# A two-level Strassen MLP: VectorE leaves its results in a free block, GpSimd adds them afterwards, and the weights' second sums are spread over the first group

## The chip, the cores and the metric

The kernel runs on one NeuronCore of a Trainium2 chip. The core has a matrix engine (TensorE, PE in the profile; PEld is its weight load), a vector engine (VectorE, DVE), a scalar engine (ScalarE, ACT), a general engine (GpSimd, POOL) and a queue that issues transfers (SyncE, SP). Each engine takes its instructions in the order in which the program has them, and they meet through semaphores. The metric is device time in microseconds (us); lower is better.

## The reference

A transformer block with cross attention, all in float32: 8 batches of 256 tokens, width 512, 16 heads, an MLP of 2048. Cut to what matters here:

```python
hidden = attention(layer_norm(x), ctx) @ cproj_w + cproj_b + x     # not touched by the change
y = layer_norm(hidden, ln2_w, ln2_b)
y = gelu(y @ fc_w + fc_b, approximate=True)    # fc_w: 512 x 2048
y = y @ proj_w + proj_b                        # proj_w: 2048 x 512
return hidden + y
```

## The kernel before, in words

**Tiling.** The 2048 tokens are four groups (`g` = 0 to 3) of 512. The attention of all groups comes first and leaves the hidden states in `hid_dram`; behind it the MLP runs group by group: for each, the fully connected layer with its GELU (tiles `pf`, results in `h`), then the projection (tiles `py`). Both parts are written out by hand: `manual_schedule` keeps every engine's instructions in the order of the source, so a line's place is its place in the queue of its engine.

**Strassen's form (with Winograd's sums).** A product of two 2 x 2 block matrices is done with seven block products in place of eight. A's sums are s1 (it is stored in the place of "21"), s2, s3, s4; B's are t1, t2, t4 and one in the place of "12". With P(a, b) for a block product: u1 = P(11,11); quarter 11 = u1 + P(12,21); u2 = u1 + P(s2,t2); u3 = u2 + P(s3,12); quarter 22 = u3 + P(21,t1); quarters 12 and 21 are u2 or u3 plus the products P(22,t4) and P(s4,22). `A_SUMS` and `B_SUMS` (summed up by L171) make the sums; `QI` gives the place of each of the seven operands in a tile.

**Group 0** uses one level. Its weights lie in four tiles `fcw[0]` to `fcw[3]`, one for each quarter `q` of the MLP's columns. For each `q`, seven `fc` products on TensorE go into PSUM banks 1, 6, 7, 5; VectorE adds make u2, u3 and the blocks of `h`, ScalarE the GELUs, and GpSimd the first two sums of `h` (`sum_h`, "s3" and "s2"). `sum_up(GP, fcw[q + 1], ...)` makes the next quarter's weight sums, `some_pw` takes steps of the generator `sum_pw`, which makes the projection weights' sums on VectorE (16 adds, 128x512 each).

**Groups 1 to 3** use two levels: each of the seven outer products is itself done with seven `sub` products of four matmuls, 128 tokens wide. An outer product `k` needs the weight operand `FC_ORDER[k][0]` as seven inner operands: these lie in `w2_dram` and are loaded to one of four tiles `w` by `load_w2`, four outer products ahead (the first four of group 1 during `py` of group 0). What has to be made for `w2_dram`, from the tiles `fcw` of group 0: the four raw inner quarters of each operand, which `keep_quarters` stores (from all seven operands at once, one transfer for each q and c, L982), and the four inner sums, which `split_sums` makes: four adds of 128x256 on VectorE or GpSimd into one of three slots of the tile `w_stage`, then two stores (L973, L974). A slot is taken again when its stores have landed. There are 14 such calls: seven operands, r = 0 (from `fcw[0]` and `fcw[2]`) and r = 1 (from `fcw[1]` and `fcw[3]`). The tile of the tokens' inner sums (`split_y`) has the same place as `w_stage`.

**The outer sums of groups 1 to 3.** `product(k, base, to)` makes four blocks, "11", "12", "21", "22", and puts them into `h[to]`, adding the blocks of `h[base]` if there is a base. For the three blocks that also get an inner u2 or u3, GpSimd first adds base and u into `h[to]` (`prepare`), and VectorE then adds the bank to that (`made`). Bank 5 is used twice in a product: `made("22")` reads it, and then `sub(5, "s4", "22", False, True)` adds to it; so TensorE can't start the latter before `made("22")` is done. After product 4, `both_to` adds whole parts of `h` to one another, half on GpSimd, half on VectorE. `h` has a fifth part, "s3": it holds the sums h11 - h21 from `sum_h("s3")` on, and in the fully connected layer of groups 1 to 3 nothing is in it.

**GELUs of groups 1 to 3.** `gelu` puts eight ScalarE instructions of a quarter into a list, and `some_gelus` issues two of them after each `sub`; ScalarE also copies u1 out of bank 1 (L1188).

**Projection, and the next group.** In `py` seven `proj` products of 32 matmuls use bank 1, 7, 1, 6, 1, 5, 7. Between them stand the next group's layer norm (`seen`, `roots`, `normalise`; L194 to L203), its transposes (`turn_next`, tile `pyt`), its sums and `split_y`; in group 0 also the second half of `split_sums` and the first `load_w2`. All adds by the helper `add` have line L927, all its matmuls L924: they are told apart by their tiles.

Of the kernel before, what the change touches and what calls it, by code (L numbers as in the profile page):

```python
# [16 lines left out]
P = 128  # L17
# [5 lines left out]
def tile_xattn_block(  # L23
# [45 lines left out]
    nc = tc.nc  # L69
# [16 lines left out]
    HI, HC, HF, HD2 = INNER // 2, NC // 2, NF // 2, D // 2  # L86
# [30 lines left out]
    at, col_of = 0, []  # L117
# [131 lines left out]
    with ExitStack() as att:  # L249
# [513 lines left out]
        g = 1  # L763
# [142 lines left out]
    with ExitStack() as mlp:  # L906
# [19 lines left out]
        def add(eng, to, a, b, op=ALU.add):  # L926
            eng.tensor_tensor(to, a, b, op)  # L927
# [9 lines left out]
        def sum_pw():  # L937
# [18 lines left out]
        w2_dram = tc.dram_tile([7, P, 7, HI // 2], F32, name="w2_dram")  # L956
        stage = wpool.tile([P, 3, 4, S], F32, tag="y2", bufs=1, name="w2_stage")
        FC_ORDER = (
            ("11", "11"), ("12", "21"), ("21", "t1"), ("s2", "t2"), ("s3", "12"), ("s4", "22"), ("22", "t4")
        )  # L960
        stages = [0]

# [11 lines left out]
            nc.sync.dma_start(to[:, 4:7, :], st[:, 1:, :])  # L974

        def keep_quarters(q):
            r = q % (NQF // 2)
            for c in range(HC):
                if q < NQF // 2 or c:
                    i = c if q < NQF // 2 else 3  # L980
                    to = w2_dram.rearrange("n p i s -> p n i s")[:, :, i, r * S : (r + 1) * S]
                    nc.sync.dma_start(to, fcw[q].t[:, :, c, :])  # L982

        w2 = {}

        def load_w2(g, k):
            t = wts.tile([P, 7, HC, S], F32, tag="w", bufs=4, name=f"w2_{g}_{k}")
            t = t.rearrange("p i h s -> p i (h s)")
            nc.sync.dma_start(t, w2_dram[QI[FC_ORDER[k][0]]])
            w2[g, k] = t  # L990

        y2s = {}
# [15 lines left out]
        for g in range(NG):  # L1008
# [39 lines left out]
            if g == 0:  # L1048
                y = ys[g]

                def fc(bank, w, b, q, first, last):
                    for i in range(2):
                        for c in range(HC):
# [5 lines left out]
                                last and c == HC - 1,  # L1059
                            )  # L1060

                for q in range(NQF):
# [16 lines left out]

                    def some_pw(n):  # L1080
                        if q:
                            for _ in range(n):
                                next(pw_sums)

                    ahead = q + 1 < NQF
                    fc(bank[1], "11", "11", q, True, False)
                    nc.scalar.copy(u1, bank[1])
                    fc(bank[6], "s2", "t2", q, True, True)
                    add(V, u2, bank[6], u1)
                    fc(bank[7], "s3", "12", q, True, False)  # L1090
                    add(V, u3, bank[7], u2)
                    fc(bank[5], "21", "t1", q, True, False)
                    add(V, x["22"], by_h(bank[5]), by_h(u3))
                    if ahead:
                        sum_up(GP, fcw[q + 1], A_SUMS, 0, 1)
                    some_pw(1)
                    fc(bank[1], "12", "21", q, False, True)

                    gelu("11", 0, by_h(bank[1]))
                    gelu("22", 1, x["22"])  # L1100
                    fc(bank[7], "22", "t4", q, False, True)
                    add(V, x["12"], by_h(bank[7]), by_h(u2))
                    if ahead:
                        sum_up(GP, fcw[q + 1], A_SUMS, 2, 3)
# [4 lines left out]
                    some_pw(1)  # L1109
# [6 lines left out]
                    if q == 2:  # L1116
                        split_sums(V, "11", 0)
                        split_sums(V, "12", 0)
                        for k in range(3):
                            keep_quarters(k)  # L1120
                    if q == 3:
                        split_sums(V, "21", 0)
                        split_sums(GP, "s2", 0)
                        split_sums(V, "s3", 0)
                        split_sums(GP, "s4", 0)
                        split_sums(V, "22", 0)
                        keep_quarters(3)
                        bias_ht()
            else:
                gelus = []  # L1130

                def some_gelus(n=2):
                    for f in gelus[:n]:
                        f()
                    del gelus[:n]
# [17 lines left out]
                def product(k, base, to):  # L1153

                    wt, yn = w2[g, k], QI[FC_ORDER[k][1]]
                    bank = {}
# [6 lines left out]
                    def sub(n, w, b, first, last):  # L1163
                        if first:
                            bank[n] = bank_of(n, f"pf{n}_{k}").rearrange("p i (j s) -> p (i j) s", j=2)
                        for m in range(HF // 2):
                            mm(
                                bank[n][:, m, :],
                                wt[:, QI[w], ts(m, P)],
                                y_of(b),  # L1170
                                first and m == 0,
                                last,
                            )
                        some_gelus()

                    def u(n):
                        return us(n, f"u{n}_{k}").rearrange("p i (j s) -> p (i j) s", j=2)

                    def prepare(cd, x):
                        if base:  # L1180
                            add(GP, block(to, cd), block(base, cd), x)

                    def made(cd, n, x):
                        add(V, block(to, cd), bank[n], block(to, cd) if base else x)

                    sub(1, "11", "11", True, False)
                    u1 = u(1)
# [4 lines left out]
                    prepare("21", u2)  # L1192
                    prepare("12", u2)
# [3 lines left out]
                    prepare("22", u3)  # L1197
# [3 lines left out]
                    if base:  # L1201
                        add(V, block(to, "11"), bank[1], block(base, "11"))
                    else:
                        nc.scalar.copy(block(to, "11"), bank[1])
                    sub(7, "22", "t4", False, True)
                    made("21", 7, u2)
                    sub(5, "s4", "22", False, True)
# [3 lines left out]
                    elif g + 1 < NG:  # L1211
                        load_w2(g + 1, k - 3)

                def both_to(to, x):

                    for eng, cd in ((GP, "21"), (V, "22"), (GP, "12"), (V, "11")):
                        add(eng, block(to, cd), block(to, cd), block(x, cd))


                product(0, None, "21")  # L1220
                product(1, "21", "11")
                gelu("11", 0)
                ht = residual(work, hid_dram[g], "resm", f"resm_{g}")
                load_next()
                product(2, None, "22")
                product(3, "21", "21")
                product(4, "21", "12")
                both_to("21", "22")
                both_to("22", "12")
                product(5, "21", "21")  # L1230
                gelu("21", 0)
                gelu("22", 1)
                product(6, "12", "12")
                some_gelus(len(gelus))
                gelu("12", 1)
                for which in ("s3", "s2"):
# [31 lines left out]
            u1, u2, u3 = (us(n, f"v{n}") for n in (1, 2, 3))  # L1268
            proj(bank[1], "11", "11", True, False)
            add(V, u1, bank[1], by_tiles(projb[:, HD2:]))  # L1270
            if g:
                some_gelus(HF)
            if g + 1 < NG:
                seen, roots, normalise = layer_norm(hids[g + 1], f"m{g + 1}")
# [6 lines left out]
                for f in normalise:  # L1281
                    f()
            if g == 0:
                split_sums(V, "11", 1)
                split_sums(GP, "12", 1)
                load_w2(1, 0)
                load_w2(1, 1)
            proj(bank[1], "12", "21", False, True)
            o_add(V, 0, 0, bank[1])
            for q in range(NQF):  # L1290
# [1 line left out]
            turn_next(0)  # L1292
            turn_next(1)
            if g == 0:
                split_sums(V, "21", 1)
                split_sums(GP, "s2", 1)
# [5 lines left out]
            turn_next(2)  # L1302
            turn_next(3)
            if g == 0:
                for n in ("s3", "s4", "22"):
                    split_sums(GP, n, 1)
                load_w2(1, 2)
                load_w2(1, 3)
# [57 lines left out]
```

## Time and profile before

| What | us |
|---|---|
| median of 3 runs (809.61 to 810.27) | 810.21 |
| the profiled execution | 808.85 |
| its span, from first to last instruction | 807.0 |
| TensorE busy (share of the span) | 755.3 (94%) |
| GpSimd busy | 473.0 (59%) |
| VectorE busy | 443.7 (55%) |
| ScalarE busy | 299.3 (37%) |
| attention, first `pf` matmul of group 0 at | 355.3 |
| `pf` of group 0, `py` of group 0 | 355.3 to 403.4, to 461.6 |
| `pf` of group 1, `py` of group 1 | 461.8 to 526.6, to 576.7 |
| `pf` of group 2, `py` of group 2 | 576.7 to 640.0, to 690.9 |
| `pf` of group 3, `py` of group 3 | 690.9 to 752.3, to 807.0 |

In a group of the profile, the name before `<-` is the tile written, those after it are read; then come the shape, the count, the busy time and the mean duration in ns, and behind the last bar the time the engine stood idle just before these instructions and what ended it. The page counts a float32 matmul as two records. The granted clock is a share of TensorE's full clock. A line of the time-ordered view has the start, the duration of the merged piece, engine and line, and in brackets the idle time before it with its releaser.

### The profile page before, as it was taken

Reading aid. Unit: us, or ns where it says so; the run is one execution under the profiler, and the core shown is the slowest. Engines: PE = TensorE matmul, PEld = TensorE weight load, DVE = VectorE, ACT = ScalarE, POOL = GpSimd, SP = SyncE. Lnnn points to the kernel's source line nnn. Section 1 sums busy time; section 2 is a strip of 40 time slices with the busy share of each in tenths; the row PEclk is TensorE's granted clock in tenths of the full one; section 3 lists DMA queues with packets and bytes.
Section 4 is the critical chain, followed back from the end, with each engine's and each line's share of the span. In section 5 each row is a group of like instructions: output and inputs, shape, how many; then the busy total and the mean of one; then the engine's idle time right before and its main releaser. Section 6 shows DMA issues by size and latency. Waiting matters only on the chain.

```text
span 807.0 us, 13477 instructions
## 1 busy us (share of the span) xinstructions
PE 755.3 (94%) x4941; PEld 648.0 (80%) x4941; DVE 443.7 (55%) x1085; ACT 299.3 (37%) x867; POOL 473.0 (59%) x431
## 2 busy tenths in 40 slices
PE   9999999999999999999979978799987899997997
PEld 8887777878888777788868877788987788886886
DVE  4667656755565668553779654553546353545111
ACT  3186777657767777504300012320020500021300
POOL 3866879486544789965468714594035671125940
PEclk9999999999999999999999999899998799998999
DMA  9525223713242584259395789520276400360001
GB/s 299 201 93 171 95 92 105 238 58 102 92 162 84 178 266 140 79 153 317 100 311 170 269 307 368 183 92 1 64 294 255 169 15 3 141 235 1 1 1 52
DMA packets 76449, 120.17 MB, mean 149 GB/s; under 512 B 5940, under 2 KB 59488, under 8 KB 73568
## 3 DMA queue, kind: packets, MB, share of 16 engines
q1 hardware_dynamic: 76128, 119.29, 43.4%
q8 instruction: 39, 0.64, 0.3%
q14 instruction: 26, 0.21, 0.1%
q0 software_dynamic: 256, 0.02, 0.0%
HBM read 85.48 MB, written 33.82 MB: 148 GB/s over the span
## 4 chain that ended last, share of the span: by engine, by line
PE 76%; POOL 10%; DVE 8%; DMA 2%; ACT 2%; issue 2%; SPq 0%; DVEq 0%; POOLq 0%
PE pf L924 18%; PE py L924 18%; POOL h L927 7%; PE ppt L625 6%; PE pqT L367 6%; PE pv L367 5%; PE po L367 5%; PE s L572 5%; PE pkT L367 4%; PE av L641 4%; POOL w_stage L927 2%; PE pkT L464 2%; DVE h L927 2%; DVE w_stage L927 1%; ACT pr L600 1%
## 5 line engine op out<-in xcount | busy, mean ns | idle before, releaser
L924 PE MATMUL pf<-y,w 128*128 128x128 f32 x1176 | 151.8, 294 | 38.2 <-DVE h L927 27.7
L924 PEld LDWEIGHTS pf<-y,w 128*128 128x128 f32 x1176 | 147.5, 208 | 42.4 <-DVE h L927 30.8
L614 POOL TENSOR_TENSOR pr<-pr,rsum 128x512 f32<-128x512 f32 x128 | 130.2, 1048 | 75.8 <-DVE rsum L612 44.5
L600 ACT ACTIVATE pr<-pr,nmax 128x256 f32<-128x256 f32 x256 | 128.1, 503 | 61.4 <-DVE nmax L590 61.2
L927 POOL TENSOR_TENSOR h<-h,u 128x512 f32<-128x512 f32 x45 | 55.7, 1267 | 146.3 <-DVE u L927 146.3
L590 DVE CUSTOM_DVE_ANT_0 pr<-s,mb 128x256 f32<-128x256 f32 x256 | 94.1, 413 | 42.0 <-PE s L572 35.0
L924 PE MATMUL py<-pw,h 128*128 128x256 f32 x384 | 89.0, 392 | 4.6 <-DVE v L927 4.6
L1188 ACT COPY u<-pf 128x512 f32<-128x512 f32 x21 | 12.2, 582 | 214.5 <-PE pf L924 214.5
L924 PEld LDWEIGHTS py<-pw,h 128*128 128x128 f32 x384 | 75.5, 198 | 15.7 <-DVE v L927 5.0
L924 PE MATMUL py<-pw_t,h 128*128 128x256 f32 x384 | 84.3, 379 | 0.0
L924 PEld LDWEIGHTS py<-pw_t,h 128*128 128x128 f32 x384 | 72.6, 190 | 10.0 <-DVE pw_t L927 0.3
L625 PEld LDWEIGHTS ppt<-ident,pr 128*128 128x128 f32 x512 | 57.3, 141 | 14.8 <-issue 9.5
L625 PE MATMUL ppt<-ident,pr 128*128 128x128 f32 x512 | 68.7, 276 | 0.2
L927 DVE TENSOR_TENSOR h<-pf,h 128x512 f32<-128x512 f32 x60 | 38.7, 686 | 52.0 <-POOL h L927 45.6
L1139 ACT ACTIVATE h<-h,cols 128x256 f32<-128x256 f32 x96 | 39.9, 497 | 66.5 <-DVE h L927 66.5
L927 POOL TENSOR_TENSOR h<-h,h 128x512 f32<-128x512 f32 x44 | 58.0, 1349 | 5.8 <-issue 4.7
L927 DVE TENSOR_TENSOR u<-pf,u 128x512 f32<-128x512 f32 x50 | 34.5, 690 | 40.8 <-PE pf L924 34.4
L630 ACT COPY pt<-ppt 128x512 f32<-128x512 f32 x96 | 51.6, 570 | 4.9 <-PE ppt L625 4.9
L367 PE MATMUL pv<-vw,ctxT 128*128 128x256 f32 x224 | 52.4, 380 | 0.0
L367 PE MATMUL pqT<-xnT,qw 128*128 128x256 f32 x224 | 51.0, 379 | 0.0
L924 PE MATMUL pf<-y,fcw 128*128 128x256 f32 x224 | 48.5, 379 | 0.0
L600 ACT ACTIVATION_READ_ACCUMULATOR pr<-pr,nmax 128x1 f32 x256 | 48.5, 189 | 0.0
(140 smaller groups left out, 1163.9 us busy)
## 6 DMA issues: line engine op xcount, KB each, us to landing
w<-w_dram SPq DMA_DIRECT2D x21, 1792.0 KB, 7.7
w_dram<-w_stage SPq DMA_DIRECT2D x14, 384.0 KB, 2.7
w_dram<-fcw SPq DMA_DIRECT2D x6, 896.0 KB, 9.1
ctx<-in_ctx_dram SPq DMA_DIRECT2D x16, 256.0 KB, 4.9
x<-in_x_dram SPq DMA_DIRECT2D x16, 256.0 KB, 4.5
v_dram<-st_v SPq DMA_DIRECT2D x16, 256.0 KB, 2.2
v<-v_dram SPq DMA_DIRECT2D x16, 256.0 KB, 3.5
resx<-in_x_dram SPq DMA_DIRECT2D x16, 256.0 KB, 5.1
```

Of the source, the lines that this page charges most:

```text
L367: nc.tensor.matmul(bank[n][:, i, :], l[:, c, ts(i, P)], r[:, c, :], start=first and i == 0 and c == 0, stop=last and c == HC - 1, skip_gro ...
L464: nc.tensor.matmul(bank[:, i, :], w[f"{n[0]}{j + 1}"][:, c, ts(i, P)], x()[f"{j + 1}{n[1]}"][:, c, :], start=at == 0, stop=j == 1 and c == ...
L572: nc.tensor.matmul(banks[j][:, i, :], qT[j * HD : (j + 1) * HD, b * S + i * P : b * S + (i + 1) * P], kT[j * HD : (j + 1) * HD, b * SK : ( ...
L590: nc.vector.tensor_tensor_reduce(pr[:, j, i, :], banks[j][:, i, :], mbias[g][1][:, b, :], scale=-SCALE, scalar=FLT_MAX, op0=ALU.add, op1=A ...
L600: nc.scalar.activation(pr[:, j, i, :], pr[:, j, i, :], AF.Exp, bias=nmax[:, j, i : i + 1], scale=-1.0, accum_out=sums[:, j, i : i + 1],)
L614: nc.gpsimd.tensor_tensor(pr[:, j], pr[:, j], rsum[:, j, :, None].to_broadcast([P, NQ, SK]), ALU.mult,)
L625: nc.tensor.transpose(ps[:, kc, ts(i, P)], probs[n][:, j, i, ts(kc, P)], ident)
L630: nc.scalar.copy(pt, ps)
L641: nc.tensor.matmul(av[j * HD : (j + 1) * HD, :], vs[g, hg][:, b * NK + kc, ts(j, HD)], pts[n, j][:, kc, :], start=(kc == 0), stop=(kc == N ...
L924: nc.tensor.matmul(ps, lhsT, rhs, start=first, stop=last, skip_group_check=True)
L927: eng.tensor_tensor(to, a, b, op)
L1139: nc.scalar.activation(h[n][:, :, p, :], h[n][:, :, p, :], AF.Gelu_apprx_tanh, bias=col(c_fcb, half * HF + p), scale=1.0,)
```

## The change

- `product` no longer adds base and u ahead. For the blocks "12", "21", "22" VectorE adds the bank and u into `r`, one of four slots of `h["s3"]`, and GpSimd afterwards adds `r` and the base to the target, for each of a list of (target, base) pairs. So u2 and u3 are read by VectorE alone. Block "11" is still added by VectorE, from the bank, once for each pair. Where a product has no base (product 0), the blocks go to the target as before.
- The order of the outer products is another, such that each result is the one before plus one product: 21 = P0; 11 = 21 + P1; 21 += P2; 12 = 21 + P3; 22 = 12 + P4 and 21 += P4; 21 += P5; 12 += P6. `both_to` falls away. Product 2, which had no base, now has one.
- `some_gelus` issues three at a time, and stands behind u2, behind u3, ahead of each `made` and ahead of block "11"; it no longer stands between the first `sub` and the copy of u1.
- The 14 `split_sums` are placed anew: ten in quarters 2 and 3 of group 0, after u2, u3 and the third block of a quarter (table `SPLITS`; six of the ten on GpSimd, four on VectorE), four in `py` of group 0. Before, seven were at the ends of quarters 2 and 3 and seven in `py`.
- The weight sums `A_SUMS` of `fcw[1]` and `fcw[2]` are made in quarter 0, those of `fcw[3]` in quarter 1; before, each in the quarter ahead of its own. The 16 steps of `pw_sums` are four in quarter 1, two in quarter 2, two in quarter 3, and two times four in `py`.
- `keep_quarters` stores only the operands "21", "s2", "s3", "s4" (two transfers in place of one), at the ends of quarters 1, 2 and 3. For "11", "12" and "22", `load_w2` takes the raw inner quarters from `fc_w` itself: five transfers in place of one, of the same bytes.

```diff
         FC_ORDER = (
-            ("11", "11"), ("12", "21"), ("21", "t1"), ("s2", "t2"), ("s3", "12"), ("s4", "22"), ("22", "t4")
+            ("11", "11"), ("12", "21"), ("s2", "t2"), ("s3", "12"), ("21", "t1"), ("s4", "22"), ("22", "t4")
         )
...
-                    nc.sync.dma_start(to, fcw[q].t[:, :, c, :])
+                    nc.sync.dma_start(to[:, 4:7], fcw[q].t[:, 4:7, c, :])
+                    nc.sync.dma_start(to[:, 2], fcw[q].t[:, 2, c, :])
...
-            nc.sync.dma_start(t, w2_dram[QI[FC_ORDER[k][0]]])
+            n = FC_ORDER[k][0]
+            src = w2_dram[QI[n]]
+            if n in ("11", "12", "22"):
+                m, c = int(n[0]) - 1, int(n[1]) - 1
+                rows = fc_w.rearrange("(c p) n -> p c n", p=P)[:, c * HC : (c + 1) * HC]
+                for to, cc, half in ((0, 0, 0), (1, 1, 0), (3, 1, 1)):
+                    at = m * HI + half * HI // 2
+                    nc.sync.dma_start(t[:, to], rows[:, cc, at : at + HI // 2])
+                nc.sync.dma_start(t[:, 2], src[:, 2])
+                nc.sync.dma_start(t[:, 4:7], src[:, 4:7])
+            else:
+                nc.sync.dma_start(t, src)
...
+                SPLITS = {
+                    (2, 0): ((GP, "11", 0), (V, "12", 0)),
+                    (2, 1): ((GP, "s2", 0),),
+                    (2, 2): ((V, "s3", 0), (GP, "21", 0)),
+                    (3, 0): ((GP, "s4", 0), (V, "22", 0)),
+                    (3, 1): ((GP, "11", 1),),
+                    (3, 2): ((V, "12", 1), (GP, "s2", 1)),
+                }
...
-                        if q:
-                            for _ in range(n):
-                                next(pw_sums)
-
-                    ahead = q + 1 < NQF
+                        for _ in range((0, n, n // 2, n // 2)[q]):
+                            next(pw_sums)
+
+                    fc_sums = [(1, 0), (1, 1), (1, 2), (1, 3)] if q == 0 else []
+                    fc_sums += [(q + 2, i) for i in range(4)] if q + 2 < NQF else []
...
                     add(V, u2, bank[6], u1)
+                    splits(q, 0)
                     fc(bank[7], "s3", "12", q, True, False)
                     add(V, u3, bank[7], u2)
+                    splits(q, 1)
                     fc(bank[5], "21", "t1", q, True, False)
                     add(V, x["22"], by_h(bank[5]), by_h(u3))
-                    if ahead:
-                        sum_up(GP, fcw[q + 1], A_SUMS, 0, 1)
-                    some_pw(1)
+                    some_fc_sums(4)
+                    some_pw(2)
+                    splits(q, 2)
...
-                    def prepare(cd, x):
-                        if base:
-                            add(GP, block(to, cd), block(base, cd), x)
-
                     def made(cd, n, x):
-                        add(V, block(to, cd), bank[n], block(to, cd) if base else x)
+                        some_gelus()
+                        if sums[0][1] is None:
+                            add(V, block(sums[0][0], cd), bank[n], x)
+                            return
+
+                        r = h["s3"][:, parts[0] % 4 // 2, parts[0] % 2 * HF // 2 :][:, : HF // 2]
+                        parts[0] += 1
+                        add(V, r, bank[n], x)
+                        for to, base in sums:
+                            add(GP, block(to, cd), block(base, cd), r)
...
-                product(0, None, "21")
-                product(1, "21", "11")
+                product(0, ("21", None))
+                product(1, ("11", "21"))
                 gelu("11", 0)
                 ht = residual(work, hid_dram[g], "resm", f"resm_{g}")
                 load_next()
-                product(2, None, "22")
-                product(3, "21", "21")
-                product(4, "21", "12")
-                both_to("21", "22")
-                both_to("22", "12")
-                product(5, "21", "21")
+                product(2, ("21", "21"))
+                product(3, ("12", "21"))
+                product(4, ("22", "12"), ("21", "21"))
+                product(5, ("21", "21"))
                 gelu("21", 0)
                 gelu("22", 1)
-                product(6, "12", "12")
+                product(6, ("12", "12"))
...
-            if g:
+            if g == 0:
+                load_w2(1, 0)
+                split_sums(V, "s3", 1)
+                split_sums(GP, "21", 1)
+                load_w2(1, 1)
+            else:
                 some_gelus(HF)
...
             if g == 0:
-                split_sums(V, "11", 1)
-                split_sums(GP, "12", 1)
-                load_w2(1, 0)
-                load_w2(1, 1)
+                split_sums(GP, "s4", 1)
+                split_sums(V, "22", 1)
+                load_w2(1, 2)
+                load_w2(1, 3)
```

More of the change, by code (lines that the diff above doesn't have):

```diff
@@ L1060, in fc, with splits @@
                             )
+                SPLITS = {
[6 more added lines that the diff above has]
+                }
+                def splits(q, at):
+                    for args in SPLITS.get((q, at), ()):
+                        split_sums(*args)
                 for q in range(NQF):
@@ L1080, in some_pw, with some_fc_sums @@
                     def some_pw(n):
-                        if q:
-                            for _ in range(n):
-                                next(pw_sums)
-                    ahead = q + 1 < NQF
+                        for _ in range((0, n, n // 2, n // 2)[q]):
+                            next(pw_sums)
+                    fc_sums = [(1, 0), (1, 1), (1, 2), (1, 3)] if q == 0 else []
+                    fc_sums += [(q + 2, i) for i in range(4)] if q + 2 < NQF else []
+                    def some_fc_sums(n):
+                        for at, i in fc_sums[:n]:
+                            sum_up(GP, fcw[at], A_SUMS, i)
+                        del fc_sums[:n]
                     fc(bank[1], "11", "11", q, True, False)
@@ L1102, in tile_xattn_block @@
                     add(V, x["12"], by_h(bank[7]), by_h(u2))
-                    if ahead:
-                        sum_up(GP, fcw[q + 1], A_SUMS, 2, 3)
+                    some_fc_sums(4)
                     some_pw(2)
@@ L1108, in tile_xattn_block @@
                     add(V, x["21"], by_h(bank[5]), by_h(u2))
-                    some_pw(1)
                     gelu("21", 0, x["21"])
@@ L1115, in tile_xattn_block, with some_gelus @@
                         load_next()
[L1116 to L1120, printed above, removed]
-                    if q == 3:
[L1122 to L1127, printed above, removed]
+                    if q >= 1:
+                        keep_quarters(q)
+                    if q == 1:
+                        keep_quarters(0)
+                    if q == 3:
                         bias_ht()
             else:
-                gelus = []
-                def some_gelus(n=2):
+                gelus, parts = [], [0]
+                def some_gelus(n=3):
                     for f in gelus[:n]:
@@ L1151, in block, with product @@
                     return h[n][:, d, c * HF // 2 : (c + 1) * HF // 2, :]
-                def product(k, base, to):
+                def product(k, *sums):
                     wt, yn = w2[g, k], QI[FC_ORDER[k][1]]
@@ L1173, in sub @@
                             )
-                        some_gelus()
                     def u(n):
                         return us(n, f"u{n}_{k}").rearrange("p i (j s) -> p (i j) s", j=2)
-                    def prepare(cd, x):
-                        if base:
-                            add(GP, block(to, cd), block(base, cd), x)
                     def made(cd, n, x):
-                        add(V, block(to, cd), bank[n], block(to, cd) if base else x)
+                        some_gelus()
[7 more added lines that the diff above has]
+                            add(GP, block(to, cd), block(base, cd), r)
                     sub(1, "11", "11", True, False)
@@ L1191, in product @@
                     add(V, u2, bank[6], u1)
-                    prepare("21", u2)
-                    prepare("12", u2)
+                    some_gelus()
                     sub(7, "s3", "12", True, False)
@@ L1196, in product @@
                     add(V, u3, bank[7], u2)
-                    prepare("22", u3)
+                    some_gelus()
                     sub(5, "21", "t1", True, False)
@@ L1200, in product @@
                     sub(1, "12", "21", False, True)
[L1201 to L1204, printed above, removed]
+                    some_gelus()
+                    for to, base in sums:
+                        if base:
+                            add(V, block(to, "11"), bank[1], block(base, "11"))
+                        else:
+                            nc.scalar.copy(block(to, "11"), bank[1])
                     sub(7, "22", "t4", False, True)
@@ L1212, in product @@
                         load_w2(g + 1, k - 3)
-                def both_to(to, x):
-                    for eng, cd in ((GP, "21"), (V, "22"), (GP, "12"), (V, "11")):
-                        add(eng, block(to, cd), block(to, cd), block(x, cd))
-                product(0, None, "21")
-                product(1, "21", "11")
+                product(0, ("21", None))
+                product(1, ("11", "21"))
                 gelu("11", 0)
@@ L1270, in tile_xattn_block @@
             add(V, u1, bank[1], by_tiles(projb[:, HD2:]))
-            if g:
+            if g == 0:
[3 more added lines that the diff above has]
+                load_w2(1, 1)
+            else:
                 some_gelus(HF)
@@ L1294, in tile_xattn_block @@
             if g == 0:
-                split_sums(V, "21", 1)
-                split_sums(GP, "s2", 1)
+                for _ in range(4):
+                    next(pw_sums)
             proj(bank[6], "21", "t2", True, True)
@@ L1304, in tile_xattn_block @@
             if g == 0:
[L1305 to L1308, printed above, removed]
+                for _ in range(4):
+                    next(pw_sums)
             bank[3] = bank_of(1, "py3")
```

## The prediction

> **What bounds the kernel now.** I read the page's own chain first, then the costliest groups, then TensorE alone in order of time over one group of the fully connected layer, last a table of stages. The chain:
>
> ```profile
> PE 76%; POOL 10%; DVE 8%; DMA 2%; ACT 2%; issue 2%; SPq 0%; DVEq 0%; POOLq 0%
> ```
>
> TensorE is the chain for three quarters of the span; what can be gained is in the 20% of GpSimd, VectorE and DMA. Where they sit:
>
> ```profile
> L924 PE MATMUL pf<-y,w 128*128 128x128 f32 x1176 | 151.8, 294 | 38.2 <-DVE h L927 27.7
> L927 POOL TENSOR_TENSOR h<-h,u 128x512 f32<-128x512 f32 x45 | 55.7, 1267 | 146.3 <-DVE u L927 146.3
> L927 DVE TENSOR_TENSOR h<-pf,h 128x512 f32<-128x512 f32 x60 | 38.7, 686 | 52.0 <-POOL h L927 45.6
> ```
>
> A circle: TensorE stands 27.7 us for VectorE's `h`, which stands 45.6 us for GpSimd's `h`. In order of time, for group 1 (start, duration, how many matmul records, idle before and its releaser):
>
> ```profile
> 468.07 11.49 PE L924 MATMUL pf<-y,w 128*128 128x128 f32 x88 [1.39 <-DVE resm L927]
> 481.35 12.77 PE L924 MATMUL pf<-y,w 128*128 128x128 f32 x112 [1.79 <-DVE h L927]
> 495.98 6.52 PE L924 MATMUL pf<-y,w 128*128 128x128 f32 x56 [1.86 <-DVE h L927]
> 504.30 5.62 PE L924 MATMUL pf<-y,w 128*128 128x128 f32 x48 [1.80 <-DVE h L927]
> 512.09 2.08 PE L924 MATMUL pf<-y,w 128*128 128x128 f32 x8 [2.16 <-DVE u L927]
> ```
>
> A product is 56 records (7 sub-products, 4 matmuls, 2 records each). The records put the stalls inside products 1, 3, 4, 5, 6, before the last sub-product: it accumulates into bank 5, which `made("22")` must have read, and that VectorE add waits for the third of GpSimd's three `prepare` adds (476.86 to 480.57, VectorE at 480.60, TensorE at 481.35). Products 0 and 2, which have no base, run through without one. The stall of 2.16 us is product 5, whose `u2` stood behind `both_to` on VectorE.
>
> The clock is the second loss. Columns: window, its length, busy time (and count) of PE, PEld, DVE, ACT, POOL, then granted clock:
>
> ```profile
> 468.10:479.50 11.40, 11.40 (x88) 11.27 (x88) 4.66 (x7) 1.17 (x2) 2.64 (x3) 0.87 0.98 345
> 481.40:494.10 12.70, 12.70 (x112) 12.53 (x112) 6.62 (x10) 4.91 (x11) 2.61 (x3) 1.00 0.85 310
> 512.00:514.20 2.20, 2.08 (x8) 1.78 (x8) 0.03 (x1) 0.00 (x0) 2.20 (x3) 0.50 0.00 0
> ```
>
> At clock 1.00 a record takes 12.77/112 = 0.114 us; after stalls the clock falls to 0.5 for a while. The three stages (461.84 to 526.61, 576.71 to 639.98, 690.93 to 752.33) take 64.77 + 63.27 + 61.40 = 189.44 us; 392 records each at 0.114 would be 44.7, together 134.1.
>
> **The change, part by part.**
>
> (1) *Products of groups 1 to 3.* Gone: 15 `prepare` adds and 4 `both_to` adds on GpSimd, 4 `both_to` adds on VectorE (13.6 us for 12), per group. New: 18 VectorE adds bank + `u` into one of four slots in `s3`, of the form that products 0 and 2 show (`h<-pf,u`, 0.69 us), each followed by one GpSimd add, by two in product 4: 3 x 4 + 6 + 3 = 21 per group. The "11" block stays on VectorE (7 adds against 5). GpSimd: 21 x 1.27 = 26.7 us in 44.7. VectorE: 14 + 21 + 7 = 42 operations x 0.69 = 29 us. Neither binds.
>
> TensorE's wait: `made("22")` now needs only bank 5 and `u3`. Two sub-products, 2 x 0.91 us, run meanwhile, against 0.69 plus some 0.25 of hand-over: hidden with 0.9 us to spare. Where does the stall go? Results in `h` become late: GpSimd finishes a product some 2.6 us after TensorE. Its readers: the next product's bases (GpSimd itself, in order); the GELUs of h11, queued behind `u1` and `u2` of product 2, done near +5.9 of 6.4 us (8 x 0.41), so the next `u1` copy, behind them on ScalarE, isn't late; the four slots: product 4 fills GpSimd until 5.8 us into product 5, where the slot it frees last is next wanted in product 6. With the stalls goes the low clock. So 189.44 - 134.1 = **-55.3**, of it 38.2 waits (page) and about 17 clock.
>
> The Trainium skill has two rules against this. "GPSIMD Engine Reference", Engine selection, sends elementwise adds to VectorE, GpSimd being about 2x slower with two inputs. The trace agrees on price (1.27 against 0.69): if it lay on the path, 63 adds x 0.58 = 36.5 us of the 55.3 were lost, and the answer were 788. The rows give GpSimd 18 us of room per group, so I take zero. "TensorE: Matmul & The Clock Gate", Part 1, has the clock drop only after an idle window of about 3.4 us. No idle here exceeds 2.66 us, so by that rule the slow stretches aren't the stalls' doing and some 17 us stay (768). The row says otherwise: 0.50 right after 2.16 us of idle, 1.00 in the unbroken stretch. I go by the row.
>
> (2) *What is late behind these stages.* In groups 1 and 2 the sums `s3`, `s2` and `bias_ht` start when GpSimd has the last add, 2.6 us after `py` begins (before: 1.8 us ahead of it). `roots` then ends at 2.6 + 4.9 + 5.0 + 2.5 + 1.3 = 16.3, four normalisations x 1.43 = 22.1, while `turn_next(0)` is due at 3 x 6.91 = 20.7: the last of four transposes is late, about 1.1 us: **+2.2** for two groups. Against it, `py` of groups 2 and 3 begins cold today (32 matmuls in 7.76 and 7.91 us, not 6.91): **-1.85**.
>
> (3) *Group 0: the weights' second sums.* 14 `split_sums` (4 adds, 2 stores each) all stay. Twelve ran after the last quarter's matmuls (403.4), the last store at 460.3; `split_y` shares their tile, so group 1 began with 4.6 us of VectorE waiting for a store:
>
> ```profile
> 463.19 1.09 DVE L927 TENSOR_TENSOR y<-y 128x896 f32<-128x896 f32 x1 [4.62 <-DMA w_dram<-w_stage]
> 422.19 8.96 PEld L924 LDWEIGHTS py<-pw,h 128*128 128x128 f32 x32 [4.98 <-DVE v L927]
> ```
>
> The second line is TensorE behind VectorE, itself stopped by a stage slot. Now ten of the 14 are issued in quarters 2 and 3, six of them on GpSimd, which is busy 8.0 and 2.8 us of 12 there; the `A_SUMS` of quarters 2 and 3 move a quarter earlier (8 adds; quarter 0 gets 5.2 us on GpSimd, where 4.6 are free, before anything that TensorE waits for), and the 16 `pw` adds are spread anew, eight of them into `py`. On GpSimd a split costs 2.9 us alone, 3.5 beside VectorE; on VectorE 1.7 alone, 3.5 beside GpSimd (rows of `w_stage`). The new wait: VectorE's "s3" in quarter 2 takes slot 0 again, so it stands until GpSimd's "11" is stored (ends about 387.6, store 0.4 + 2.7, so 390.8 to 394.3), and "12" in quarter 3 stands for GpSimd's "s4" (stored near 406.7, done 410.2). Queued behind them on VectorE are `u3`, `x12`, `x21`, and so the bank reads and GELUs that TensorE and the `s3` sums need. Followed instruction by instruction: TensorE loses about 0.2 us in quarter 2, 2.0 in quarter 3 (bank 7, `u3` behind "22"), nothing before `py`, 1.8 at `turn_next(0)`; group 1 starts at 458.0, y ready. From below: no wait at all would be 98.3 us from 355.3, so 453.6; from above: every stage store at the 5.66 us that the chain shows for one, 464. I take 458: **-3.8**.
>
> (4) *DMA.* `keep_quarters`: 6 x 896 KB become 6 x 384 and 6 x 128 KB, 5.4 to 3.1 MB. `load_w2` of "11", "12", "22" becomes five DMAs, same bytes: 36 more issues x 0.35 us on SP, which spends 127 us waiting for TensorE; nothing. The slack shrinks, though: load 6 of a group leaves when product 2 ends (19 us), behind 2 MB of `resm` and `hm`, and has until 38; at 300 GB/s it is there by about 31. Without that cover: up to 6 us per group. The first four loads of group 1 move ahead of the late stores and land well before 458.
>
> Sum: -55.3 + 2.2 - 1.85 - 3.8 = -58.8. The profiled execution took 808.85 us (span 807.0 and 1.85 around it): 750.1. The runs' median, 810.21, lies 1.4 higher: **751.4**.
>
> **Rivals.**
> - *Clock stays low*: the page's rule; for it, the clock is also below 1 in `py` of group 0. 751.4 + 17 = 768. Chance 0.07.
> - *Group 0 gets worse*: VectorE's stage waits reach TensorE. For: two waits of 3 to 4 us are in my own chain, and store landings range from 1.7 to 9.8 us. Against: only bank 7 and `turn_next` are near. 464 to 468 in place of 458, so 757 to 762. Chance 0.17.
> - *All covered*: group 0 ends at 453.6, `turn_next` on time: 751.4 - 4.4 - 2.2 = 745. Chance 0.12.
> - *GpSimd becomes the bound, the other sign*: place, the 21 adds per group. It decides from 63.1/21 = 3.0 us per add on; at 3.3, 69 us per group and about 825. Against: 1.25 to 1.28 us over all `h<-h,u`, 1.72 at most for `h<-h,h` beside VectorE, and the new VectorE adds read PSUM, beside which no row shows GpSimd slowed. Chance 0.04.
> - *ScalarE in order*: GELUs wait for GpSimd and hold a `u1` copy; up to 3 us in two products per group, some 760 to 770. Chance 0.05.
>
> **How the numbers follow.** The forecast (751, own range 747 to 756) has 0.55. Range 744 to 767: it takes in all-covered, group 0 worse and most of ScalarE, leaving out the low clock and the GpSimd bound. Under 0.2% can't be told from no change: same 0.01, slower 0.04, faster 0.95.
>
> **What would show it.** Right: each `pf` stage of groups 1 to 3 near 45 us, clock 1.00, no `DVE h <- POOL h` wait among the longest; GpSimd `h<-h` adds 63, near 1.27 us; group 1's first matmul near 458; a gap of 1 to 2 us before `pyt`. Wrong: GpSimd adds above 2 us, `u` waiting for ACT, a `pf` stage above 50 us, or VectorE idle for `w_dram<-w_stage` with TensorE stopped behind it.

## The result, and the profile after

The changed kernel takes **745.68 us** (median of 4 runs, 745.05 to 745.91); the kernel before, in the same set of runs, 809.91 (804.89 to 810.27). The ratio is 0.922, with a 95% interval of 0.918 to 0.926: 64 us less. The forecast was 751.4 with a range of 744 to 767; the time lies in it, 1.7 us from its lower end, and 1.3 us below the narrower range, 747 to 756. The profiled execution has a span of 743.0 us, 64.0 below that of before.

The chain that ended last, and two groups of the page; behind the count stand busy time, mean ns and the idle time before:

```profile
PE 86%; DVE 5%; issue 3%; POOL 3%; ACT 2%; DVEq 0%; POOLq 0%
...
L927 POOL TENSOR_TENSOR h<-h,hs 128x512 f32<-128x512 f32 x79 | 98.6, 1276 | 108.8 <-DVE hs L927 108.5
...
L924 PE MATMUL pf<-y,w 128*128 128x128 f32 x1176 | 131.8, 275 | 0.0
```

TensorE's 38.2 us of waits in these stages are gone and its busy time fell from 151.8 to 131.8 us for the same 1176 records: 58.2 us in one line. GpSimd has as much to do as before (481.8 us busy in all, 473.0 before), but it is 3% of the chain in place of 10%. The 75 adds of the form `h<-h,hs` in the MLP's groups 1 to 3 (63 new ones and the 12 `s2` sums) take 1.275 us each: the new VectorE adds beside them don't slow them.

TensorE in order of time over group 1, then the three stages as windows (columns as in the prediction):

```profile
456.42 43.94 PE L924 MATMUL pf<-y,w 128*128 128x128 f32 x392
500.19 7.07 PE L924 MATMUL py<-pw,h 128*128 128x256 f32 x32
...
520.91 0.49 PE L216 MATMUL pyt<-ident,hm 128*128 128x128 f32 x3
522.22 0.77 PE L216 MATMUL pyt<-ident,hm 128*128 128x128 f32 x5 [0.82 <-DVE hm L203]
```

```profile
456.42:500.19 43.77, 43.77 (x394) 43.77 (x392) 28.75 (x42) 10.94 (x24) 23.71 (x19) 1.00 0.83 311
551.33:595.10 43.77, 43.77 (x393) 43.77 (x392) 28.75 (x42) 10.94 (x24) 23.69 (x19) 1.00 0.84 312
646.23:690.00 43.77, 43.77 (x393) 43.76 (x392) 28.76 (x42) 10.94 (x24) 23.69 (x19) 1.00 0.44 163
```

All 392 records of a stage are one unbroken piece, at clock 1.00, where seven to nine pieces stood. The only wait of the group is 0.82 us at the transposes. In group 0 TensorE still waits 0.73 us in quarter 3 and 0.38 + 1.08 us at the transposes; the second line is VectorE held by a stage store:

```profile
400.87 3.72 PE L924 MATMUL pf<-y,fcw 128*128 128x256 f32 x16 [0.73 <-DVE u L927]
...
405.95 0.42 DVE L927 TENSOR_TENSOR w_stage<-fcw,fcw 128x256 f32<-128x256 f32 x1 [3.23 <-DMA w_dram<-w_stage]
...
425.91 0.33 PE L216 MATMUL pyt<-ident,hm 128*128 128x128 f32 x1 [0.38 <-DVE hm L203]
427.31 0.76 PE L216 MATMUL pyt<-ident,hm 128*128 128x128 f32 x5 [1.08 <-DVE hm L203]
```

The span's 64.0 us: 58.1 from the stages of groups 1 to 3 (189.44 to 131.31), 5.4 from group 0 (group 1 begins at 456.42, not 461.84), and 0.4 from `py` (50.1, 50.95, 54.67 to 51.14, 51.13, 53.0). The second of these is the least firm: in the five runs below whose group 0 is the one of the changed kernel, group 1 begins at 456.68 to 458.83.

### The profile page after: what moved, and what is told of

Read it like the earlier page. It is cut to its first block, busy times and chain, and to the rows that moved or that the text cites. A ratio compares the mean times of both kernels' runs of the same rounds, so it can differ in the third digit from the quotient of the medians.

```text
span 743.0 us, 13604 instructions
## 1 busy us (share of the span) xinstructions
PE 731.2 (98%) x4941; PEld 628.7 (85%) x4941; DVE 434.3 (58%) x1075; ACT 297.7 (40%) x864; POOL 481.8 (65%) x441
## 4 chain that ended last, share of the span: by engine, by line
PE 86%; DVE 5%; issue 3%; POOL 3%; ACT 2%; DVEq 0%; POOLq 0%
PE pf L924 23%; PE py L924 19%; PE ppt L625 7%; PE pqT L367 7%; PE pv L367 5%; PE po L367 5%; PE s L572 5%; PE av L641 5%; PE pkT L367 5%; DVE hm L203 2%; PE pkT L464 2%; ACT pr L600 2%; POOL h L927 1%; DVE w_stage L927 1%; PE pxt L216 1%
## 5 line engine op out<-in xcount | busy, mean ns | idle before, releaser
L927 POOL TENSOR_TENSOR h<-h,hs 128x512 f32<-128x512 f32 x79 | 98.6, 1276 | 108.8 <-DVE hs L927 108.5
L924 PEld LDWEIGHTS pf<-y,w 128*128 128x128 f32 x1176 | 131.8, 192 | 0.2
L924 PE MATMUL pf<-y,w 128*128 128x128 f32 x1176 | 131.8, 275 | 0.0
L924 PE MATMUL py<-pw,h 128*128 128x256 f32 x384 | 84.9, 379 | 0.0
L924 PEld LDWEIGHTS py<-pw,h 128*128 128x128 f32 x384 | 72.5, 190 | 9.6
L924 PEld LDWEIGHTS pf<-y,fcw 128*128 128x128 f32 x224 | 42.5, 190 | 6.9 <-DVE u L927 1.1
L367 PEld LDWEIGHTS pqT<-xnT,qw 128*128 128x128 f32 x224 | 41.3, 190 | 5.6 <-POOL ctxT L171 0.7
L367 PEld LDWEIGHTS pv<-vw,ctxT 128*128 128x128 f32 x224 | 41.0, 190 | 5.4 <-ACT xnT L341 0.3
```

The source lines that it names most:

```text
L367: nc.tensor.matmul(bank[n][:, i, :], l[:, c, ts(i, P)], r[:, c, :], start=first and i == 0 and c == 0, stop=last and c == HC - 1, skip_gro ...
L924: nc.tensor.matmul(ps, lhsT, rhs, start=first, stop=last, skip_group_check=True)
```

## The experiments

The theory: the time was TensorE waiting inside a product for VectorE, which waited for GpSimd, and the low clock that followed those waits; GpSimd's work moved behind the result costs nothing as long as it keeps up. The rivals: the low clock has another cause; GpSimd is close to being the bound; VectorE would do the adds better; the gain of group 0 is small, or comes from the transfers.

**The products alone.** The function `product` and the order of products from the changed kernel, all else from the kernel before.

```diff
-                product(1, "21", "11")
+                product(1, ("11", "21"))
...
-                both_to("21", "22")
-                both_to("22", "12")
```

> The products of groups 1 to 3 alone (result by VectorE into a free block, GpSimd adds afterwards, new order of products); group 0, its split sums, its stores and the weight loads are those of before. My theory: each unbroken pf stage takes 43.8 us as in the changed kernel, but group 1 still begins at 461.8 with the 4.05 us of start waits and some 1.5 us of low clock behind them; so of the 58.1 us that these stages gave, 52.6 stay, with 0.5 more from the projection: 809.9 - 53 = 757. Rival (the clock loss isn't the stalls' doing): 757 + 17 = 774. Rival (the sums of group 0 are needed for the stages to run unbroken): a stage above 50 us, 775 or more.

Measured: 758.17 us (757.64 to 758.99) against 810.4; ratio 0.935 (0.934 to 0.936). TensorE in order of time, the beginning of group 1 and the stages of groups 1 and 2:

```profile
465.84 2.04 PE L924 MATMUL pf<-y,w 128*128 128x128 f32 x8 [2.69 <-DVE y L927]
468.35 44.28 PE L924 MATMUL pf<-y,w 128*128 128x128 f32 x376 [0.47 <-DVE resm L927]
...
563.61 43.93 PE L924 MATMUL pf<-y,w 128*128 128x128 f32 x392
```

As forecast: only the start of group 1, which group 0 makes late, is broken; the other stages are whole. The clock came back with the end of the waits, with group 0 untouched: it is 1.00 from 472.6 us on, to the end of the last projection. The rival of a low clock with its own cause (774) is out.

**Everything but the products.** The complement: group 0, its stores and the loads from the changed kernel, `product` and `both_to` of before.

```diff
-                product(0, ("21", None))
-                product(1, ("11", "21"))
+                product(0, None, "21")
+                product(1, "21", "11")
```

> Everything but the products: split sums, weight sums, projection sums, stores and loads as in the changed kernel; products, both_to and GELU places of groups 1 to 3 as before. My theory: group 1 starts at 456.4 in place of 461.8 (5.4 us) and without the 4.05 us of start waits and 1.5 us of low clock: 809.9 - 10.9 = 799, and with the run of the products alone it adds up to the whole. Rival (the gain of group 0 is given back in the stages of before, because their stalls don't care when they start): about 804.5, 5.4 us only.

Measured: 797.46 us (797.10 to 797.55); ratio 0.983 (0.982 to 0.985). Against the 810.4 of that set the two halves give 52.2 and 12.9, together 65.2; the whole gave 64.2. They add up to within 1 us: the parts don't need each other. Group 1 starts at 457.51 without waiting, and then the old stalls return:

```profile
485.72 8.15 PE L924 MATMUL pf<-y,w 128*128 128x128 f32 x56 [1.86 <-DVE h L927]
495.37 5.62 PE L924 MATMUL pf<-y,w 128*128 128x128 f32 x48 [1.51 <-DVE h L927]
503.16 1.21 PE L924 MATMUL pf<-y,w 128*128 128x128 f32 x8 [2.16 <-DVE u L927]
506.87 8.45 PE L924 MATMUL pf<-y,w 128*128 128x128 f32 x56 [2.50 <-DVE h L927]
```

Two windows of the same run, the last wait and the records after it, show the clock (the last column but two): 0.50 in the wait, 0.51 for over 4 us of unbroken work behind it.

```profile
505.30:506.80 1.50, 0.00 (x0) 0.00 (x0) 0.68 (x2) 0.00 (x0) 0.79 (x1) 0.50 0.00 0
506.87:511.00 4.13, 4.13 (x19) 4.13 (x20) 1.83 (x3) 1.17 (x3) 0.00 (x0) 0.51 0.34 69
```

The same in the kernel before, at the wait of 2.16 us ahead of 512.09, in two windows of 3.41 us:

```profile
508.58:511.99 3.41, 1.34 (x13) 1.15 (x11) 3.31 (x5) 0.00 (x0) 0.98 (x2) 1.00 0.84 357
512.00:515.41 3.41, 2.08 (x8) 1.78 (x8) 0.39 (x2) 0.00 (x0) 3.02 (x3) 0.50 0.00 0
```

**The transfers of before**, in the changed kernel.

```diff
-                    nc.sync.dma_start(to[:, 4:7], fcw[q].t[:, 4:7, c, :])
-                    nc.sync.dma_start(to[:, 2], fcw[q].t[:, 2, c, :])
+                    nc.sync.dma_start(to, fcw[q].t[:, :, c, :])
...
+            nc.sync.dma_start(t, w2_dram[QI[FC_ORDER[k][0]]])
```

> The changed kernel with the transfers of before: keep_quarters stores all seven operands (5.4 MB), load_w2 loads each operand in one transfer from the kept copy. My theory: transfers are covered, 745.7 within 1.5 us. Rival (the smaller stores are what lets the stage stores land in time): VectorE's waits for stage stores grow by 3 us or more each, group 1 starts at 460 or later, 749 to 753.

Measured: 749.86 us (749.20 to 751.10); ratio 0.925 (0.923 to 0.927). My theory missed; the rival has it. VectorE and TensorE in quarters 2 and 3, in order of time:

```profile
394.05 0.43 DVE L927 TENSOR_TENSOR w_stage<-fcw,fcw 128x256 f32<-128x256 f32 x1 [5.29 <-DMA w_dram<-w_stage]
...
396.45 5.45 PE L924 MATMUL pf<-y,fcw 128*128 128x256 f32 x24 [1.51 <-DVE h L927]
404.38 5.41 PE L924 MATMUL pf<-y,fcw 128*128 128x256 f32 x16 [2.48 <-DVE u L927]
```

The stores of quarter 1 stand in the same queue ahead of the first stage stores. With four transfers of 896 KB there, VectorE's "s3" waits 5.29 us where it waits 1.32 in the changed kernel (at most 2.08 in the other runs with its group 0); the median landing of a stage store is 3.5 us, not 2.6. Block x12 and then u3 are late behind it, TensorE waits 1.51 and 2.48 us, the 16 records after that take 5.41 us in place of 3.72, and group 1 begins at 461.14, 4.7 us later: about as late as before the change (461.84), and 2.3 us or more later than in any other run with the new places. That doesn't make the new places worthless without the smaller stores: the run of the products alone, with the old places and the same transfers, took 758.17 us in the same set, 8.3 us more, because its group 1 also starts with 2.69 and 0.47 us of waits and a low clock. The loads were undone with them, but their first issue is at 419.75, behind these delays; a run with the stores alone wasn't made.

**GpSimd slower**, with one more pass over each block, and with two (`range(2)`).

```diff
+        one = wpool.tile([P, HF // 2, 1], F32, name="one")
+        nc.gpsimd.memset(one, 1.0)
...
+                        for _ in range(1):
+                            add(GP, r, r, one.to_broadcast([P, HF // 2, P]), ALU.mult)
                         for to, base in sums:
                             add(GP, block(to, cd), block(base, cd), r)
```

> The changed kernel with one more GpSimd pass over each of the 18 blocks that VectorE leaves (times one, about 1.05 us), ahead of its adds: 21 x 1.27 + 18 x 1.05 = 45.6 us of GpSimd per group in a stage of 43.8. My theory: the four slots let TensorE run the stage nearly unbroken while GpSimd falls some 8 us behind, and the loss shows up in py: the s3 sums and the layer norm's roots are late by it, 5 us in front of the s3 projection and 3 in front of the transposes; 765 (755 to 775). Rival (only the sum over the stage counts): 2 us per group, 751. Rival (GpSimd is nowhere near the path): 746.

Measured: 776.09 us (775.63 to 776.15); ratio 0.959 (0.956 to 0.962).

> The same with two more passes: 64.5 us of GpSimd per group. My theory: GpSimd is the bound; the slots fill and TensorE waits in the stage; 26 to 30 us per group, 830 (815 to 840), slower than the kernel before. Rival (half hidden by py): below 800.

Measured: 836.57 us (836.44 to 838.57); ratio 1.034 (1.030 to 1.039), slower than before the change. In the run with one more pass, TensorE in order of time behind the stage of group 1:

```profile
500.19 1.16 PE L924 MATMUL pf<-y,w 128*128 128x128 f32 x8 [0.31 <-DVE hs L927]
501.18 7.07 PE L924 MATMUL py<-pw,h 128*128 128x256 f32 x32
514.75 9.25 PE L924 MATMUL py<-pw,hs 128*128 128x256 f32 x32 [6.49 <-POOL hs L927]
```

The stage itself is nearly whole (the slots cover it), and the loss comes due where the `s3` sums are read: 6.49 us of waiting and 9.25 us for 32 records that take 7.07 at clock 1.00. (The page counts two records for a matmul here too: a `proj` product is 16 matmuls, not 32.) The first of the two places forecast was right (5 us forecast). The second wasn't: at the transposes of group 1 TensorE waits 1.41 us, not 3. What made the size (765) too small is the low clock behind the long wait, 2.2 to 2.7 us per group. Of 18.9 us more GpSimd work per group, 10.1 came through (30.4 us in three groups); of the next 18.9, 20.2 did. So the room was about 9 us per group, not the 18 that the prediction took from 44.7 - 26.7: GpSimd's first add of a group begins only when product 1 has its first result, 10.8 us into the stage (467.21), and its last must be done soon after the end. In the changed kernel that stretch is 35.6 us (467.21 to 502.83), and the 21 adds take 26.8 of it: 8.8 are left. Estimated on a straight line between these two runs, the time of before (64 us more) is reached at some 29 us of extra work per group, or 2.7 us per add in place of 1.27; the prediction said 3.0.

**VectorE adds.**

```diff
-                            add(GP, block(to, cd), block(base, cd), r)
+                            add(V, block(to, cd), block(base, cd), r)
```

> The changed kernel with the 21 adds per group on VectorE in place of GpSimd, at the same places. My theory: VectorE has 42 x 0.65 + 21 x 0.61 = 40 us in 43.8, but product 4 has 8.2 us in 6.3, so TensorE waits some 1 to 2 us per group there; the s3 sums of GpSimd come earlier and the gap ahead of the transposes closes (1.6 us): 748 (744 to 753). Rival (elementwise adds belong on the faster engine): 740 to 744.

Measured: 748.67 us (748.23 to 751.03); ratio 0.926 (0.922 to 0.929). As forecast, and not faster. In order of time: the last sums of product 4 on VectorE, u2 and u3 of product 5 behind them, and TensorE:

```profile
492.68 0.69 DVE L927 TENSOR_TENSOR hs<-pf,u 128x512 f32<-128x512 f32 x1
493.40 1.29 DVE L927 TENSOR_TENSOR h<-h,hs 128x512 f32<-128x512 f32 x2
494.61 1.48 DVE L927 TENSOR_TENSOR u<-pf,u 128x512 f32<-128x512 f32 x2
496.14 2.05 PE L924 MATMUL pf<-y,w 128*128 128x128 f32 x16 [1.42 <-DVE u L927]
```

Product 4 has two sums for each block. TensorE waits 1.42 us in each group and the stage takes 45.45 us (458.83 to 504.28), not 43.77; the gap at the transposes of groups 1 and 2 falls from 0.82 to 0.24. The slower engine is the better place, because it isn't the one that feeds TensorE. The medians stem from different sets, and the intervals of the ratios overlap; the traces are the firmer ground: from the first matmul of group 1 to the end this run takes 290.4 us, the changed kernel 286.6.

**One slot.**

```diff
-                        r = h["s3"][:, parts[0] % 4 // 2, parts[0] % 2 * HF // 2 :][:, : HF // 2]
+                        r = h["s3"][:, 0, : HF // 2]
```

> The changed kernel with one slot for VectorE's results in place of four. My theory: in products with one sum the add is done before the slot is wanted, or within 1 us, which TensorE doesn't see; in product 4 each block holds the slot for two adds, and u2, u3 of product 5 are late: 2 to 3 us per group, 753 (749 to 757). Rival (slots don't matter): 746. Rival (every block waits, as with the prepare adds before): 770 or more.

Measured: 762.58 us (761.21 to 765.70); ratio 0.943 (0.939 to 0.946): in the direction of the first theory, outside its bounds. Product 4, u2 and u3 of product 5 and TensorE, in order of time:

```profile
492.81 0.69 DVE L927 TENSOR_TENSOR hs<-pf,u 128x512 f32<-128x512 f32 x1 [2.60 <-POOL h L927]
493.42 1.48 DVE L927 TENSOR_TENSOR u<-pf,u 128x512 f32<-128x512 f32 x2
494.95 1.16 PE L924 MATMUL pf<-y,w 128*128 128x128 f32 x8 [1.74 <-DVE u L927]
496.85 7.59 PE L924 MATMUL pf<-y,w 128*128 128x128 f32 x64 [0.74 <-DVE hs L927]
```

The place is the one forecast, 3.4 us in groups 1 and 3. Group 2 loses 5.2: the same two waits, 1.74 and 0.74 us, are followed there by 64 records in 9.04 us, not 7.59. Windows of 3.4 us show the clock (columns as above), the first from group 1, the others from group 2:

```profile
492.06:495.46 3.40, 1.66 (x15) 1.47 (x14) 1.98 (x3) 0.00 (x0) 2.60 (x3) 1.00 0.99 377
...
594.46:597.86 3.40, 1.65 (x12) 1.46 (x13) 2.09 (x4) 0.00 (x0) 2.60 (x3) 1.00 0.49 201
597.88:601.27 3.39, 3.39 (x18) 3.39 (x18) 1.23 (x3) 0.50 (x1) 2.05 (x2) 0.50 0.41 101
```

TensorE is busy just under half of the time in both, and in group 2 alone the clock is halved for the next 3.4 us. The rest is what hadn't been counted: with one slot the hand-over between the engines lies in each block's path, VectorE waits for GpSimd 11 times in group 1 (12.9 us), GpSimd's last add ends 4.4 us behind the stage, not 2.6, and the gap at the transposes grows (`py` of group 1 takes 52.99 us, not 51.14).

**A different order.** Four steps moved, to close the gaps that the changed kernel has left.

```diff
-                    (3, 0): ((GP, "s4", 0), (V, "22", 0)),
-                    (3, 1): ((GP, "11", 1),),
+                    (3, 0): ((GP, "s4", 0),),
+                    (3, 1): ((V, "22", 0), (GP, "11", 1)),
...
-                split_sums(V, "s3", 1)
-                split_sums(GP, "21", 1)
-                load_w2(1, 1)
...
             if g + 1 < NG:
                 seen, roots, normalise = layer_norm(hids[g + 1], f"m{g + 1}")
                 for f in (*seen, roots):
                     f()
+            if g == 0:
+                split_sums(V, "s3", 1)
+                load_w2(1, 1)
             for q in range(NQF):
                 sum_h("s1", q)
+            if g:
+                bias_ht()
...
+                split_sums(GP, "21", 1)
                 split_sums(GP, "s4", 1)
```

> The changed kernel with four steps in another order: VectorE's split 22 of quarter 3 behind u3 instead of ahead of it; in the projection of group 0 the layer norm's statistics ahead of VectorE's split s3, and GpSimd's split 21 behind the s1 sums; in groups 1 to 3 the bias of the residual behind the layer norm's roots and the s1 sums. My theory: the gaps of TensorE that are left (0.73 in quarter 3, 1.46, 0.82 and 0.81 ahead of the transposes) close, 745.7 - 3.8 = 742. Rival (what is moved back comes due itself: s4 sums or the next tokens' sums late): a new gap of 1 to 3 us, 744 to 746.

Measured: 741.97 us (741.31 to 742.65); ratio 0.915 (0.914 to 0.916), the fastest version. TensorE in order of time, group 0 and the transposes of group 1:

```profile
433.74 1.03 PE L924 MATMUL py<-pw,h 128*128 128x256 f32 x4
435.19 1.13 PE L924 MATMUL py<-pw,h 128*128 128x256 f32 x4 [0.42 <-POOL h L927]
436.87 5.81 PE L924 MATMUL py<-pw,h 128*128 128x256 f32 x24 [0.54 <-POOL h L927]
...
520.82 1.04 PE L216 MATMUL pyt<-ident,hm 128*128 128x128 f32 x8
```

The median bears out the theory; the trace bears it out in half. In groups 1 and 2 the gap at the transposes is gone (`py` takes 50.10 us each, 51.1 in the changed kernel). In group 0 the rival is right: the gap at the transposes closed, but two GpSimd splits now stand ahead of the `s4` sums, the projection that reads these waits, and group 1 starts at 456.33, only 0.09 us earlier, which is less than the 2.4 us by which this start differs between runs with the same group 0. The profiled spans are 2.2 us apart, the medians 3.7: the profiled execution is the slowest of the four here and the fastest of the four of the changed kernel. The two ran in different sets, but the intervals of their ratios don't overlap: that it is faster is shown, by how much only roughly.

What wasn't tried: the three parts of the new `product` one by one, the free block, the order of the products and the places of the GELUs (the one-slot run bears on the first alone); GELUs at their old places, ahead of the copy of u1, in the changed kernel; and the last GpSimd split behind the `s4` sums.

## Why the prediction was right, by its own steps

- **(1) Products, -55.3 forecast, -58.1 measured.** The mechanism was right in each part: no wait for bank 5, no sum late for its reader, GELUs in time, VectorE 28.75 and ScalarE no bound. The term that was mis-sized is the time per record: 0.114 us came from dividing a piece's 12.77 us by its 112 records, but a piece has ends that don't belong to the rate (its last record alone lasts 0.275 us). Two pieces at clock 1.00 that the prediction shows give the rate without their ends, (12.77 - 5.62)/(112 - 48) = 0.1117, and the measured rate is 43.77/392 = 0.1117. That is 0.93 us per stage, 2.8 in all, and half of the whole miss.
- **The clock rule.** I set the row (0.50 behind 2.16 us of idle) above the Trainium skill's rule, "TensorE: Matmul & The Clock Gate", Part 1, an idle window of some 3.4 us. The products alone settle it: when the waits went, the clock was 1.00 throughout the stages of groups 2 and 3. That the clock drops "only" after an idle window was my reading; the same Part also tells of short idle times between groups of matmuls that make the clock swing. The traces show what counts. In all ten profiled executions the clock changes in steps of 3.41 us, and half clock lasts one to four of them; that section's freely running window fits. But the step need not be idle. In the kernel before, TensorE was busy 1.34 of the 3.41 us that end at 511.99, with most of one wait of 2.16 us at their end, and the clock was 0.50 for the next two steps, to 518.82. Over all ten, half clock followed every full-clock step in which TensorE was busy less than 42% and none with 49% or more; the one-slot run's 1.65 and 1.66 us of 3.40 lie at the upper end of the stretch between, in which both happen. So a wait well below 3.4 us can halve the clock, and where it falls in the step decides.
- **The rule on engines.** "GPSIMD Engine Reference", Engine selection, would have put the adds on VectorE. The price is as it says (1.275 us against 0.69), the choice was right against it, and the VectorE run shows why. My reason, 18 us of room on GpSimd, was too generous: it was 9.
- **(2) Behind the stages, +0.35 forecast, -0.4 measured.** `roots` ends 16.2 us into `py` (516.43 - 500.19; 16.3 forecast), the transposes wait 0.82 and 0.81 us (1.1 forecast), and groups 2 and 3 begin warm.
- **(3) Group 0, -3.8 forecast, -5.4 measured.** The waits came where they were worked out: VectorE's "s3" began at 390.07 (390.8 forecast), "12" of quarter 3 at 405.95 (406.7); TensorE stood 0.73 us in quarter 3 (2.0) and 1.46 at the transposes (1.8). Splits beside each other took 3.2 to 3.7 us (3.5 taken), so what was too large are TensorE's waits. The 458.0 forecast for the start of group 1 lies within what the runs with this group 0 show, 456.42 to 458.83. In the two latest the waits at the transposes were 0.76 or 0.84 and 1.08 us, and 32 records behind them took 8.76 us in place of 7.07: the clock again.
- **(4) Transfers, forecast nothing.** This step was wrong as an account, though not in the sum, which had taken 2.7 us per stage store, the median landing in the kernel before. At the new places it takes the smaller stores to get that: with the large ones, 4.2 us are lost. It should have stood in (3) as a cover, with the price if it is gone.

Of the rivals, "all covered" named 745, next to the result, but not what happened: its gaps didn't vanish. "GpSimd becomes the bound" had the right place and a decision point close to what the doubled passes show (2.7 us per add, 3.0 forecast).

## What to carry to other kernels

When TensorE waits for an add that itself waits for a slower engine, turn the order round: the engine that frees the bank writes into a spare block at once, and the slow one adds from there, with enough slots for the product that has the most sums. Count the slow engine's room from its first possible start to the moment its last result is read, not as the stage's length less its work. And when small stores have to land before an engine goes on, look at what stands ahead of them in the same queue.

## What I hadn't expected of the hardware

In the stages of the kernel before the clock cost about half as much as the waits (1176 records took 20.0 us more than after the change, beside 38.2 us of waiting), and it is uneven: 64 records took 7.59 or 9.04 us behind the same two waits, and 32 records 9.25 in place of 7.07 behind one wait of 6.49 us. And two sums on VectorE of 128x512, both operands in SBUF, follow each other at 0.61 us where GpSimd is idle (the run with the adds on VectorE); beside GpSimd's adds in the projection of group 0 of the changed kernel four of them took 4.90 us.
